# Two state-space layers on one core: scans in another order, one more PSUM bank for the first layer's decays, and an MLP cut by hidden features

## The chip, the core and the metric

One core of a Trainium2 chip runs the whole program. The metric is the device time of one execution in microseconds (us). All data is fp32. The engines are named as the profile names them: PE (matmul) with PEld (its weight loads), DVE (vector), ACT (activations), POOL (GpSimd) and SP, which here only issues DMAs. Each engine works through its own queue in order; an instruction that waits holds up all that is queued behind it.

## The reference, cut to what matters

The input is 8 images of 384 channels and 32 x 32 pixels. Four layers follow each other, each on the group-normalized image, each added to its input. Layers 0 and 2 are selective state-space layers over the 1024 pixels; layer 2 has a layer norm ahead and an MLP behind. Layer 1 is a filter in 8 x 8 patches with a gated depthwise convolution, layer 3 a 3 x 3 depthwise convolution.

```python
x = x + L0(gn(x)); x = x + L1(gn(x)); x = x + L2(gn(x)); x = x + L3(gn(x))

# L0 and L2, for each image: 768 inner channels d, 16 states n, 1024 places t
xin, z = split(xseq @ in_proj.T)
u   = silu(causal_conv3(xin))
dt, B, C = split(u @ x_proj.T)
dt  = softplus(dt @ dt_proj.T + bias)
dA  = exp(dt[:, :, None] * A)                     # the decay
h_t = dA_t * h_(t-1) + (dt_t * u_t) * B_t         # the scan
y_t = sum_n(h_t * C_t) + u_t * D
out = (y * silu(z)) @ out_proj.T

# L2 only
xseq = layer_norm(xseq)                            # ahead of in_proj
out  = gelu(out @ mlp_w1.T + b1) @ mlp_w2.T + b2   # 384 -> 1536 -> 384
```

## The kernel before

**Chunks and steps.** An image's 1024 places are two halves of T = 512, so each of the two state-space layers has 16 chunks. What the code calls `l0_` and `l2_` is here the first and the second layer. A chunk has 24 steps; 32 chunks give 768 steps. A step treats 32 channels with 16 states each, as four groups j = 0 to 3 of 128 partitions x 512 places. The main loop (line 1015) runs over the steps.

**What a step does.** `begin` loads dt * u from DRAM, spread to all 16 states, into a tile g, three steps ahead. `times` multiplies g by B on POOL (L623, two instructions), one step ahead. `decay` copies dt to the states with four matmuls (lhsT `selr`) into four PSUM banks dA0 to dA3 and takes the exponential in place on ACT (L241). `scan` runs four scans on DVE (L643). For j = 0 and 1 the result goes back into the dA bank and DVE multiplies it by C (L654); for j = 2 and 3 it goes into g, and one POOL instruction multiplies both by C (L660). `gather` sums over the states with four matmuls into the bank y, adds u * D with one more matmul in the first layer (the diagonal matrix is loaded once, `w_D`) or on DVE in the second, and multiplies by the gate z on DVE.

**PSUM.** There are eight banks: dA0 to dA3 (`psa`), y (`psy`), and a pool of three (`psg`, tag `ps`) that all other work shares. That work writes a pool tile with matmuls, and an ACT or DVE instruction reads it out, after which the bank is free.

**Other work.** Generators, called jobs, do the rest in pieces: `measure` and the group statistics, `front` (normalization, in_proj as ps_in, the convolution taps on DVE, x_proj, dt as ps_dt), `gates` (ps_z), `out_proj`, `layer1` (ps_t, ps_dw, ps_o1), `mlp` (ps_up, ps_dn) and `layer3`. In each step the loop emits, in this order, `times` of the next step, `scan`, job pieces of up to 2.0 units of PE work, `gather` of the step before, `begin`, more job pieces as long as the budget `ROOM` lasts, and `decay` of the next step. A piece that finds no free pool bank or no lock reports WAIT and is tried later; `jobs.until` forces pieces at once where a step needs their result. As everything is emitted in this order, a DVE instruction of a job stands behind the scans of the step in which it is emitted. Matmuls are emitted by one helper, activations by another, so the profile shows L177 and L241 for nearly all of them, and L85 for DVE work of jobs; the tile names tell them apart.

**dt.** `step_dt` takes a pool bank, computes log(1 + exp(-|x|)) on ACT into a tile `spm`, adds max(x, 0) on DVE, which frees the bank, multiplies by u on POOL into a tile `du`, and spills that to DRAM. `spm` has two buffers, which `measure` (its image blocks `xk`) and `layer_norm` (its squares `sq`) use as well; `live["spm"]` is set while `measure` uses them.

**MLP.** It runs twice over a chunk, for 256 places each time. Each pass needs all weights: 12 loads of 384 KB into four buffers `mw`, so 24 a chunk. A pool bank holds two hidden blocks of 256 places.

Of the kernel before, what the change touches and what calls it, by code (L numbers as in the profile page):

```python
# [47 lines left out]
NBANK = 3  # L48

SHARE = {"l0_": ((2, 2, 2, 2), (2, 2, 2, 2)), "l2_": ((2, 2, 2, 2), (2, 2, 2, 2))}  # L50
# [105 lines left out]
def tile_conv_preact_d4(ctx: ExitStack, tc: tile.TileContext, a: dict, out: bass.AP):  # L156
# [6 lines left out]
    psg = ctx.enter_context(tc.tile_pool(name="psg", bufs=NBANK, space=PSUM))  # L163
# [3 lines left out]
    live = {"ps": 0, "dt": 0, "x": 0, "spm": False}  # L167
# [11 lines left out]
    def ps_tile(name):  # L179

        while live["ps"] >= NBANK:
            yield WAIT
        live["ps"] += 1
        return psg.tile([P, 512], F32, tag="ps", name=name)

    def ps_done():
        live["ps"] -= 1

    def pipe(units, deep=2):
# [4 lines left out]
        while units or flying:  # L194
# [7 lines left out]
            if units and live["ps"] < NBANK and len(flying) < deep:  # L202
                went = True
                name, stages = units.popleft()
                live["ps"] += 1
                ps = psg.tile([P, 512], F32, tag="ps", name=name)
                stages[0](ps)
                f = {"stages": deque(stages[1:]), "ps": ps, "bank": True}
                settle(f)
                if f["stages"]:  # L210
                    flying.append(f)
# [3 lines left out]
    def settle(f):  # L215
        if f["bank"] and (not f["stages"] or f["stages"][0] is None):
            f["bank"] = False
            ps_done()
# [61 lines left out]
    def group_stats(block, all_read=lambda: None, between=None):  # L280
# [15 lines left out]
        def group_mean(v):  # L296
# [11 lines left out]
            return ps[:, 0:KC].unsqueeze(2)  # L308

        ps = yield from group_mean(mv[:, :, 0:1])  # L310
        nmean = wk.tile([P, KC, 1], F32, tag="gnm", name="gnm", bufs=2)
        act(nmean, ps, AF.Copy, scale=-1.0)
        ps_done()
# [5 lines left out]
        ps = yield from group_mean(dv)  # L319
        rstd = wk.tile([P, KC, 1], F32, tag="grstd", name="grstd", bufs=3)  # L320
        rsqrt(rstd, ps, eps_gn)
        ps_done()
# [33 lines left out]
    def load_diagonal(w, pre):  # L356
        w["D"] = wk.tile([P, ND, P], F32, tag="w_D", name="w_D")
        nc.sync.dma_start(w["D"], a[pre + "D"].rearrange("d p q -> p d q"))

# [4 lines left out]
    def depthwise(pool, rows, todo):  # L364
# [13 lines left out]
        for q, (n, t) in enumerate(taps):  # L378
# [8 lines left out]
            if t == 8:  # L387
                take(ps[:rows])
                ps_done()
# [9 lines left out]
    def measure(s):  # L399
# [4 lines left out]
        def load(q):  # L404
            if q < len(blocks):
                h, k = blocks[q]
                x = loaded[h, k] = wk.tile([P, T], F32, tag="spm", name="xk", bufs=2)
# [4 lines left out]
        live["spm"] = True  # L412
# [7 lines left out]
        def all_read():  # L420
            live["spm"] = False
# [38 lines left out]
    def layer_norm(xn):  # L460
# [5 lines left out]
        ps_done()  # L466
        yield NEXT
        while live["spm"]:
            yield WAIT
        ps = yield from ps_tile("ps_lv")  # L470
        for k in range(KC):
            sq = wk.tile([P, T], F32, tag="spm", name="sq", bufs=2)
            act(sq, xn[:, k, :], AF.Square)
            mm(ps, ln_mean, sq, start=k == 0, stop=k == KC - 1)
# [6 lines left out]
        ps_done()  # L481
# [5 lines left out]
    def front(s):  # L487
# [67 lines left out]
        ps_done()  # L555
# [10 lines left out]
        def step_dt(d):  # L566
# [3 lines left out]
            def log(ps):  # L570
                mm(ps, w["dt"][DT0:RX, d * P : (d + 1) * P], dbc[DT0:RX, :])
                v = got["m"] = wk.tile([P, T], F32, tag="spm", name="spm", bufs=2)
# [8 lines left out]
            def times_u(ps):  # L581
                v = got["du"] = wk.tile([P, T], F32, tag="du", name="du", bufs=2)
                nc.gpsimd.tensor_mul(v, s["dt"][d], u[d])

            def spill(ps):
# [3 lines left out]
                for j in range(4):  # L589
                    nc.sync.dma_start(to[:, j, :], got["du"][32 * j : 32 * (j + 1), :])  # L590
# [5 lines left out]
        flying = []  # L596
        for d in range(ND):
            while live["dt"] >= NDT or live["spm"]:
                yield WAIT
            live["dt"] += 1  # L600

            flying.append(pipe([("ps_dt", step_dt(d))]))
            flying = [f for f in flying if next(f, f) is not f]
            yield NEXT
        while flying:
            flying = [f for f in flying if next(f, f) is not f]
            yield NEXT
# [11 lines left out]
    def times(s, i):  # L619

        for j in (0, 2):
# [5 lines left out]
    def decay(s, i):  # L627
        k, sub = QUADS[i]
# [5 lines left out]
        for j in range(4):  # L634
            act(dAs[j], dAs[j], AF.Exp, scale=s["w"]["A"][:, 4 * i + j : 4 * i + j + 1])

    def scan(s, i):

        g = s["g", i]
        own = SHARE[s["pre"]][s["c"]][i % NSUB]  # L640
        for j in range(4):
            q = 4 * i + j
            nc.vector.tensor_tensor_scan(  # L643
                dAs[j] if j < own else g[:, j, :],
                dAs[j],
# [5 lines left out]
            if j < own:  # L651
                if s["c"] < NCH - 1:
                    nc.vector.tensor_copy(carry[:, q : q + 1], dAs[j][:, T - 1 : T])
                nc.vector.tensor_mul(g[:, j, :], dAs[j], s["bc"][:, 1, :])  # L654
        if s["c"] < NCH - 1:
            nc.vector.tensor_copy(  # L656
                carry[:, 4 * i + own : 4 * i + 4].unsqueeze(2), g[:, own:4, T - 1 : T]
            )
        g = g[:, own:4, :]
        nc.gpsimd.tensor_mul(  # L660
            g, g, s["bc"][:, 1, :].unsqueeze(1).to_broadcast([P, 4 - own, T])
        )

    def gather(s, i):
# [6 lines left out]
        for j in range(4):  # L671
            mm(y[32 * j : 32 * (j + 1), :], sely[:, sub, :], g[:, j, :], sub == 0, sub == NSUB - 1 and s["pre"] == "l2_")
        if sub == NSUB - 1:
            u = s["u"][k // NH][:, k % NH, :]
            if s["pre"] == "l0_":
                mm(y, s["w"]["D"][:, k, :], u, start=False)
# [74 lines left out]
    def load_layer1():  # L751
# [14 lines left out]
        ps_done()  # L766
# [95 lines left out]
    TH = T // 2  # L862
# [10 lines left out]
    def weights():  # L873

        parts = [a["l2_mlp_w1"][f : f + 2].rearrange("f p k q -> p f k q") for f in range(0, NF, 2)]
        parts += [
            a["l2_mlp_w2"][m][:, g * NFH : (g + 1) * NFH, :]
            for m in range(KC)
            for g in range(2)
        ]  # L880
        parts = deque(parts + parts)
# [14 lines left out]
    def mlp(s):  # L896
        x = s["x"]
        loaded, more = s["weights"]
        first = True

        def take():

            nonlocal first
            if not first:
                more()
            first = False
# [272 lines left out]
```

## Time and profile before

| | |
|---|---|
| Median of 3 runs | 7783.18 us (7766.74 to 7798.79) |
| The profiled execution | 7774.96 us, span 7773.2 us |
| Granted PE clock, mean | 0.922 |
| PE busy | 7244.1 us (93%) |
| DVE busy | 5787.0 us (74%) |
| POOL busy | 5638.8 us (73%) |
| ACT busy | 4034.0 us (52%) |
| Head, up to the first scan | 95 us |
| First layer, 384 steps | 3453 us |
| Second layer, 384 steps | 4034 us |
| Tail after the last step's first scan | 192 us |

The page is one execution. "Busy" of PE is modelled: a matmul counts from its start to the end of its write, so waits between the matmuls of a group can lie inside it. PEld rows are weight loads; a wait of PE shows there first, since the load precedes the matmul. A row of the waits reads: engine, tile and line that waited, what ended the wait, total us, how often, and the longest. A granted clock of 1.0 is full speed, 0.5 half. The first three rows of matmuls, four 32-row or 32-column matmuls at once, are the dA and y groups; a 512-column fp32 matmul appears as two instructions.

### The profile page before, as it was taken

Reading aid. Unit: us, or ns where it says so; the run is one execution under the profiler, and the core shown is the slowest. Engines: PE = TensorE matmul, PEld = TensorE weight load, DVE = VectorE, ACT = ScalarE, POOL = GpSimd, SP = SyncE. Lnnn points to the kernel's source line nnn. Section 1 sums busy time; section 2 is a strip of 40 time slices with the busy share of each in tenths; the row PEclk is TensorE's granted clock in tenths of the full one; section 3 lists DMA queues with packets and bytes.
Section 4 is the critical chain, followed back from the end, with each engine's and each line's share of the span. In section 5 each row is a group of like instructions: output and inputs, shape, how many; then the busy total and the mean of one; then the engine's idle time right before and its main releaser. Section 6 shows DMA issues by size and latency. Waiting matters only on the chain. (4 is left out here: it accounts for less than half of the span.)

```text
span 7773.2 us, 76689 instructions
## 1 busy us (share of the span) xinstructions
PE 7244.1 (93%) x25762; PEld 3001.0 (39%) x25762; DVE 5787.0 (74%) x7350; ACT 4034.0 (52%) x6980; POOL 5638.8 (73%) x2710
## 2 busy tenths in 40 slices
PE   7989999999999999999999989999999999999998
PEld 2223333333333333333334434444444444444445
DVE  5988788888777878778746765767777677776871
ACT  4445555554554555455545544555555555555543
POOL 5888878788787878778646764767767677676770
PEclk8888889999888999988899999999999999999999
DMA  5666556556565646556536654666656666565662
GB/s 141 141 151 144 138 134 142 136 135 150 127 146 127 141 120 148 128 139 146 129 78 167 174 135 120 165 156 172 165 150 174 155 170 164 149 164 146 171 168 67
DMA packets 288919, 1122.50 MB, mean 144 GB/s; under 512 B 37386, under 2 KB 90970, under 8 KB 190220
## 3 DMA queue, kind: packets, MB, share of 16 engines
q1 hardware_dynamic: 288524, 1117.59, 58.4%
q8 instruction: 204, 3.34, 0.2%
q14 instruction: 191, 1.56, 0.1%
HBM read 1041.96 MB, written 75.50 MB: 144 GB/s over the span
## 5 line engine op out<-in xcount | busy, mean ns | idle before, releaser
L623 POOL TENSOR_TENSOR g<-g,bc 128x1024 f32<-128x1024 f32 x1536 | 3586.8, 2358 | 197.2 <-DMA g<-dud 181.2
L660 POOL TENSOR_TENSOR g<-g,bc 128x1024 f32<-128x1024 f32 x768 | 1806.2, 2352 | 1441.1 <-DVE carry L656 806.6
L241 ACT ACTIVATE dA<-dA,w_A 128x512 f32<-128x512 f32 x3072 | 1860.7, 662 | 1543.3 <-PE dA L177 1530.1
L177 PE MATMUL dA<-dt,selr 32*128 32x512 f32 x6144 | 1573.3, 677 | 70.6 <-DVE g L654 61.9
L643 DVE TENSOR_TENSOR_SCAN dA<-dA,carry,g 128x512 f32<-128x512 f32 x768 | 986.6, 1285 | 616.0 <-issue 275.6
L643 DVE TENSOR_TENSOR_SCAN dA<-dA,g 128x512 f32<-128x512 f32 x768 | 940.6, 1225 | 477.5 <-issue 167.7
L654 DVE TENSOR_TENSOR g<-dA,bc 128x512 f32<-128x512 f32 x1536 | 1053.9, 686 | 29.8 <-DVE dA L643 0.5
L177 PE MATMUL y<-g,sely 128*32 128x512 f32 x6144 | 934.1, 637 | 43.0 <-POOL g L660 37.5
L643 DVE TENSOR_TENSOR_SCAN g<-dA,carry,g 128x512 f32<-128x512 f32 x768 | 940.6, 1267 | 0.0
L643 DVE TENSOR_TENSOR_SCAN g<-dA,g 128x512 f32<-128x512 f32 x768 | 893.3, 1204 | 0.0
L177 PEld LDWEIGHTS dA<-dt,selr 32*128 32x128 f32 x6144 | 470.2, 191 | 984.4 <-DVE g L643 517.3
L177 PE MATMUL ps_dn<-h,mw 128*128 128x256 f32 x2304 | 573.9, 401 | 75.3 <-DMA mw<-in_l_mlp_w 58.6
L177 PE MATMUL ps_up<-t,mw 128*128 128x256 f32 x2304 | 566.8, 394 | 59.0 <-DMA mw<-in_l_mlp_w 44.2
L177 PE MATMUL ps_z<-xf,w_in 128*128 128x512 f32 x1152 | 586.1, 649 | 27.3 <-DVE dt L85 23.6
L177 PE MATMUL ps_in<-xf,w_in 128*128 128x512 f32 x1152 | 566.9, 633 | 27.3 <-DVE u L85 25.5
L177 PE MATMUL ps_dw<-tp,diag 96*96 96x512 f32 x1152 | 572.8, 638 | 15.2 <-ACT diag L241 15.2
L177 PE MATMUL ps_out<-u,w_out 128*128 128x512 f32 x1152 | 543.7, 619 | 10.2 <-DVE x L85 10.2
L177 PEld LDWEIGHTS ps_dn<-h,mw 128*128 128x128 f32 x2304 | 439.5, 197 | 277.0 <-issue 118.8
L177 PEld LDWEIGHTS ps_up<-t,mw 128*128 128x128 f32 x2304 | 425.8, 192 | 268.4 <-issue 148.9
L177 PE MATMUL ps_dw<-xp,diag 128*128 128x512 f32 x864 | 407.5, 622 | 42.2 <-ACT diag L241 40.9
L241 ACT ACTIVATE u<-ps_in,w_vec 128x512 f32<-128x512 f32 x192 | 149.4, 778 | 484.2 <-PE ps_in L177 484.2
L177 PEld LDWEIGHTS y<-g,sely 128*32 128x32 f32 x6144 | 134.2, 111 | 648.5 <-issue 461.1
(99 smaller groups left out, 6463.1 us busy)
## 6 DMA issues: line engine op xcount, KB each, us to landing
g<-dud SPq DMA_DIRECT2D x768, 1024.0 KB, 7.1
mw<-in_l_mlp_w SPq DMA_DIRECT2D x384, 384.0 KB, 7.4
dud<-du SPq DMA_DIRECT2D x768, 64.0 KB, 1.7
xk<-in_x SPq DMA_DIRECT2D x48, 256.0 KB, 4.2
xf<-in_x SPq DMA_DIRECT2D x16, 768.0 KB, 8.4
x<-in_x SPq DMA_DIRECT2D x16, 768.0 KB, 8.5
x_mid<-x SPq DMA_DIRECT2D x16, 768.0 KB, 4.6
xk<-x_mid SPq DMA_DIRECT2D x48, 256.0 KB, 5.0
```

The costliest lines, as they stand in the source:

```text
L177: nc.tensor.matmul(out_, lhsT, rhs, start=start, stop=stop)
L241: nc.scalar.activation(out_, in_, func, **kw)
L623: nc.gpsimd.tensor_mul(g, g, s["bc"][:, 0, :].unsqueeze(1).to_broadcast([P, 2, T]))
L643: nc.vector.tensor_tensor_scan(dAs[j] if j < own else g[:, j, :], dAs[j], g[:, j, :], 0.0 if s["c"] == 0 else carry[:, q : q + 1], ALU.mul ...
L654: nc.vector.tensor_mul(g[:, j, :], dAs[j], s["bc"][:, 1, :])
L660: nc.gpsimd.tensor_mul(g, g, s["bc"][:, 1, :].unsqueeze(1).to_broadcast([P, 4 - own, T]))
```

## The change

Six edits, which belong to three groups.

- **Decays and scans.** The order of groups in a step is now 2, 3, 0, 1 for the exponentials and the scans, and `times` treats j = 2, 3 first. POOL's product by C is emitted right after scan 3. In the first layer the exponential of group 1 is taken last in a step (`decay_last`) and goes from its dA bank into a bank of its own, `dAx` (tag `b2`), where scan 1 and its product work. The matmuls keep the order 0, 1, 2, 3. The pool has two banks, `b0` and `b1`, in the first layer; `b2` joins them after the last step of the first layer. The diagonal of D is made on ACT from the unit matrix, 96 times, and is loaded no more.
- **MLP.** It runs over all 512 places at once and is cut by hidden features: six blocks up, GELU, down into x; then the other six. Each weight is loaded once a chunk. A pool bank holds one hidden block, and a piece is one matmul of 512 columns.
- **Squares and dt.** The three squares of `layer_norm` are taken one step ahead of the matmuls that sum them; `spm` has three buffers, `du` is gone (the product is written into `spm`), and `live["spm"]` names who holds the buffers: `measure`, `squares` or `dt`.

```diff
-NBANK = 3
+OWN = 2
+ORDER = (2, 3, 0, 1)
...
-    live = {"ps": 0, "dt": 0, "x": 0, "spm": False}
+    live = {"dt": 0, "x": 0, "spm": None, "banks": ["b0", "b1"]}
...
+    def bank(name):
+        tag = live["banks"].pop(0)
+        ps = psg.tile([P, 512], F32, tag=tag, name=name)
+        held[id(ps)] = ps, tag
+        return ps
+
+    def ps_done(ps):
+        live["banks"].append(held.pop(id(ps))[1])
...
+        live["spm"] = "squares"
+        sq = [wk.tile([P, T], F32, tag="spm", name="sq", bufs=3) for _ in range(KC)]
+        for k in range(KC):
+            act(sq[k], xn[:, k, :], AF.Square)
+        yield NEXT
         ps = yield from ps_tile("ps_lv")
         for k in range(KC):
-            sq = wk.tile([P, T], F32, tag="spm", name="sq", bufs=2)
-            act(sq, xn[:, k, :], AF.Square)
-            mm(ps, ln_mean, sq, start=k == 0, stop=k == KC - 1)
+            mm(ps, ln_mean, sq[k], start=k == 0, stop=k == KC - 1)
+        live["spm"] = None
...
             def times_u(ps):
-                v = got["du"] = wk.tile([P, T], F32, tag="du", name="du", bufs=2)
-                nc.gpsimd.tensor_mul(v, s["dt"][d], u[d])
+                nc.gpsimd.tensor_mul(got["m"], s["dt"][d], u[d])
...
     def times(s, i):
-        for j in (0, 2):
+        for j in (2, 0):
...
-        for j in range(4):
-            act(dAs[j], dAs[j], AF.Exp, scale=s["w"]["A"][:, 4 * i + j : 4 * i + j + 1])
+        s["dA"] = list(dAs)
+        for j in ORDER:
+            if j != ORDER[-1] or s["pre"] == "l2_":
+                act(dAs[j], dAs[j], AF.Exp, scale=s["w"]["A"][:, 4 * i + j : 4 * i + j + 1])
+
+    def decay_last(s, i):
+        if s["pre"] == "l0_":
+            j = ORDER[-1]
+            s["dA"][j] = psg.tile([P, T], F32, tag="b2", name="dAx")
+            act(s["dA"][j], dAs[j], AF.Exp, scale=s["w"]["A"][:, 4 * i + j : 4 * i + j + 1])
...
     def scan(s, i):
-        for j in range(4):
+        for j in ORDER:
...
-            if j < own:
+            if j < OWN:
                 if s["c"] < NCH - 1:
-                    nc.vector.tensor_copy(carry[:, q : q + 1], dAs[j][:, T - 1 : T])
-                nc.vector.tensor_mul(g[:, j, :], dAs[j], s["bc"][:, 1, :])
-        if s["c"] < NCH - 1:
-            nc.vector.tensor_copy(
-                carry[:, 4 * i + own : 4 * i + 4].unsqueeze(2), g[:, own:4, T - 1 : T]
-            )
-        g = g[:, own:4, :]
-        nc.gpsimd.tensor_mul(
-            g, g, s["bc"][:, 1, :].unsqueeze(1).to_broadcast([P, 4 - own, T])
-        )
+                    nc.vector.tensor_copy(carry[:, q : q + 1], dA[j][:, T - 1 : T])
+                nc.vector.tensor_mul(g[:, j, :], dA[j], s["bc"][:, 1, :])
+            elif j == 3:
+                if s["c"] < NCH - 1:
+                    nc.vector.tensor_copy(
+                        carry[:, 4 * i + OWN : 4 * i + 4].unsqueeze(2), g[:, OWN:4, T - 1 : T]
+                    )
+                r = g[:, OWN:4, :]
+                nc.gpsimd.tensor_mul(
+                    r, r, s["bc"][:, 1, :].unsqueeze(1).to_broadcast([P, 4 - OWN, T])
+                )
...
+        if sub == NSUB - 2 and s["pre"] == "l0_":
+            s["D", k] = wk.tile([P, P], F32, tag="D", name="D")
+            act(s["D", k], eye, AF.Copy, scale=s["w"]["vec"][:, k, 4:5])
...
-                mm(y, s["w"]["D"][:, k, :], u, start=False)
+                mm(y, s.pop(("D", k)), u, start=False)
...
     def weights():
...
+        for g in range(2):
+            for f in range(g * NFH, (g + 1) * NFH, 2):
+                parts.append(a["l2_mlp_w1"][f : f + 2].rearrange("f p k q -> p f k q"))
+            for m in range(KC):
+                parts.append(a["l2_mlp_w2"][m][:, g * NFH : (g + 1) * NFH, :])
...
-        for half in range(2):
-            cols = slice(half * TH, (half + 1) * TH)
-            h1 = p2.tile([P, NF, TH], F32, tag="h1", name="h1")
+        for g in range(2):
+            h1 = p2.tile([P, NFH, T], F32, tag="h1", name="h1")
...
+                def run(k):
+                    def run_k(ps):
+                        if f % 2 == 0 and k == 0:
+                            take()
+                        mm(
+                            ps, now[0][:, f % 2 * KC + k, :], s["t"][k], start=k == 0,
+                            stop=k == KC - 1,
+                        )
...
+                    xm = x[:, m, :]
+                    if g == 0:
+                        vector.scalar_tensor_tensor(
+                            xm, ps, b2[:, m : m + 1], xm, ALU.add, ALU.add
+                        )
+                    else:
+                        vector.tensor_add(xm, ps, xm)
...
         scan(s, i)
+        if t == total // 2 - 1:
+            live["banks"].append("b2")
...
         jobs.step(t)
-        if t + 1 < total:
-            decay(*steps[t + 1])
+        if nxt:
+            decay(*nxt)
+            decay_last(*nxt)
```

## The prediction

> **What bounds the kernel now.** I read the busy rows of the page, then the busy times by stretch (head, first layer, second layer, tail; the cuts are the first scans of the layers), then the waits inside each layer, then the instructions in order of time.
>
> The busy times by stretch, columns PE, PEld, DVE, ACT, POOL, granted clock, DMA:
>
> ```profile
> 95.00:3547.80 3452.80, 3262.05 (x10780) 1131.25 (x10780) 2835.17 (x3561) 1815.44 (x3218) 2810.77 (x1348) 0.90 0.58 138
> 3547.80:7581.50 4033.70, 3758.78 (x14333) 1743.26 (x14332) 2912.64 (x3726) 2122.07 (x3581) 2808.05 (x1343) 0.95 0.61 154
> ```
>
> PE looks full, but its matmuls are modelled to last until they end, stalls included. What it streams can be counted: dense 512-column fp32 matmuls are two instructions whose starts lie 0.43 us apart (0.86 us in all), a quad of dA or y takes 1.07 to 1.13 us. With these the program's PE work is 6.40 us a step in the first layer and 8.34 us in the second, of 9.0 and 10.5 us that a step lasts. DVE does 6.25 us of scans and products in each step and 1.3 to 1.5 us of other work. So PE and DVE are nearly equal, each 70 to 87% used, and the time is lost where they wait for each other. The waits of the first layer, then of the second:
>
> ```profile
> PEld dA L177 <- DVE g L643: 308.6, 430, 1.7
> PEld dA L177 <- DVE g L654: 180.5, 140, 13.1
> PEld ps_z L177 <- DVE dt L85: 34.2, 13, 5.3
> ```
> ```profile
> PEld dA L177 <- DVE g L643: 207.8, 309, 1.7
> PEld ps_lv L177 <- ACT sq L241: 65.8, 43, 4.6
> PE ps_dn L177 <- DMA mw<-in_l_mlp_w: 58.6, 24, 5.6
> PE ps_up L177 <- DMA mw<-in_l_mlp_w: 44.2, 34, 4.8
> PE ps_lv L177 <- ACT sq L241: 37.2, 13, 3.0
> ```
>
> The dA matmuls write over the banks that the scans still read, so PE stands some 490 us in the first layer behind scans and products. In the other direction, DVE idles between the steps for 555 us in the first layer and 1053 us in the second (counted from the end of one step's scans to the first scan of the next, less the DVE work between), nearly all of it ended by the first exponential, thus by a PE that came late. From the first dA matmul to the first scan takes 1.9 us.
>
> One step in order of time, where a bank of the pool is at fault:
>
> ```profile
> 2572.93 2.45 DVE L643 TENSOR_TENSOR_SCAN g<-dA,carry,g 128x512 f32<-128x512 f32 x2
> ...
> 2575.30 0.67 DVE L85 SCALAR_TENSOR_TENSOR dt<-ps_dt,spm 128x512 f32<-128x512 f32 x1
> ...
> 2576.02 5.36 PE L177 MATMUL ps_z<-xf,w_in 128*128 128x512 f32 x6 [4.38 <-DVE dt L85]
> ...
> 2581.31 1.14 PE L177 MATMUL dA<-dt,selr 32*128 32x512 f32 x8
> ...
> 2583.21 1.29 DVE L643 TENSOR_TENSOR_SCAN dA<-dA,carry,g 128x512 f32<-128x512 f32 x1 [6.32 <-POOL g L623]
> ```
>
> ps_z needs the bank that ps_dt held. Its release is the dt addition on DVE, which is queued behind all four scans of the step. PE idles 4.38 us, then works at half speed (six matmuls in 5.36 us instead of 2.6), and only then come the dA matmuls: the step is 14.1 us long. DVE stands from 2576.9 to 2583.2.
>
> **What the Trainium skill says.** "TensorE: Matmul & The Clock Gate", Part 1: after an idle window of about 3.4 us PE runs at half its clock until it has been busy again for about as long. The lines above agree (0.86 us from ps_z to ps_z after 4.38 us idle). "Perfetto Trace Analysis", Matmuls: independent groups should rotate through different PSUM banks so that the eviction of one overlaps the next. "PSUM — Partial Sum Buffer", Specifications: eight banks, each 512 fp32 columns. The kernel has 4 (dA) + 1 (y) + 3 (pool), so the first layer's extra bank can only come out of the pool, which keeps two.
>
> **The change part by part.**
>
> First layer, decays and scans. Now the order on DVE is scan 2, scan 3, scan 0, product 0, scan 1, product 1. dA0 is free after product 0, that is 1.9 us (1.24 + 0.69) before the step's end; dA1 is free once the exponential into the extra bank is done; dA2 and dA3 have long been free. PE can thus pass the dA matmuls up to 1.9 us earlier. Exponential 2 starts 1.16 us after them and scan 2 0.75 us later, just when product 1 ends, so DVE loses nothing. The gather that follows needs product 1; in the changed program's order it comes first in 192 of 382 steps, and there the lead is only the 1.1 us of the quad. Per step, the smaller of PE's present stall, this lead, and the DVE idle time that follows it: 124 us over the layer where the lead is carried from step to step and steps with a bank wait are left out, 171 us with the full lead everywhere. I take -145. The exponential last in the step waits for product 1 on ACT; behind it are the next step's evictions, whose matmuls end later than it does (ACT is 53% busy), so nothing. POOL's product now needs two scans instead of four; POOL is the last to release a step's first scan in 3 of 383 steps, so nothing. The new diagonal on ACT, 96 x 0.40 = 38 us, has a step of room: nothing; without that room at most 38.
>
> Pool of two banks in the first layer, single f per bank in the MLP. In the built order I looked for PE work that stands behind a DVE eviction of its own step, hence behind all its scans, as ps_z above. Before: 15 steps in the first layer and 23 in the second; after: 78 and 68, mostly ps_t, ps_o1 and ps_up behind dt. PE work left behind the wait, up to the dA matmuls: 70 and 153 us before, 270 and 363 after. Such a gap is about that work plus 1.5 us (0.7 eviction + 1.9 - 1.1 for the quad counted). Set against the gap that the same steps have now (they average 3.7 and 4.4 us, so many are late already) this adds 69 + 71 = 140 us. The upper end: steps of this kind lose 4.4 us against 9.0 with 3.6 us of work behind (six, ps_z), 1.3 us with 1.8 (four, ps_t), 1.0 us with 2.4 in the second layer (thirteen, ps_up), half clock included; drawn on to the others it gives about 430. I take +200, nearer the low end, because a PE that is late does not wait.
>
> Order in the second layer. There is no extra bank: dA1 waits for product 1, the end of the step, and dA2 is issued behind it. So each gap is at least 2.0 us, which 97 steps now undercut by 92 us in sum. Some of that meets a late PE: +55 (0 to 92).
>
> MLP. Streaming is equal: 216 ns from start to start for 256 columns, 429 for 512; weight loads run under it. Weights are loaded once, 12 pieces of 384 KB a chunk instead of 24, and each lasts 5.1 us of PE instead of 2.6, so three pieces ahead cover 15 us, over the 7.4 us to landing. The gaps before ps_up and ps_dn with a mark over 0.5 us sum to 128 us; the two DMA lines above hold 103. -110 (80 to 128). Pieces of one matmul fill the steps better: five forced stretches of 32.9 us of PE work become 20.1, three more lose 14 in all, 78 us together; the work moves into steps that are about half full of it: -45 (0 to 78). Evictions: ACT 384 x 0.47 becomes 192 x about 0.65, hidden; DVE 96 adds of 0.47 become 96 of about 0.70, +22 us, half exposed: +10.
>
> Squares a step ahead: three squares of 0.64 us end before PE comes. Idle PE before ps_lv 37 us plus 3 in the first layer: -40 (20 to 65, the weight-load line). The dt buffers (du into spm) and the missing load of w_D lie under other work: nothing, at most 5.
>
> Sum: -145 + 200 + 55 - 110 - 45 + 10 - 40 = -75. The profiled execution took 7774.96 us with a span of 7773.2; the median 7783.18 is 8 above. 7775 - 75 + 5 = 7705.
>
> **The rivals.**
> A, slower: the bank waits decide. Speaking for it: the six ps_z steps, and that PE, when it leads, only waits longer and goes cold. At 430 us the sum is +155: 7935. It decides from 275 us on, which is 2.5 us for each of the 108 added steps. Against it: the 140 us of the first working.
> B, no change: the lead is not used, since in the first layer the next thing PE meets waits for the step's end anyway (half of the steps open with the gather, 65 with ps_dt). 40 instead of 145: sum +30, 7810.
> C, much faster: bank waits at 140, lead carried further with fewer half-clock stretches (these cost 280 us in the first layer now): lead -250, sum -240 with the rest as above: 7545.
>
> **How the numbers follow.** Forecast 0.40, A 0.25, B 0.20, C 0.15. About 0.5% (39 us) is what a measurement of this kernel can tell from no change. The forecast's own range is 7630 to 7760. Faster: most of the forecast's (0.34), all of C, a little of B (0.04): 0.53. Slower: A and 0.04 of B: 0.29. The rest, 0.18, is the same. The range from 7540 to 7940 reaches to C and A.
>
> **What would show it.** Right: PE's waits for scans before dA in the first layer fall from 490 us to under 300, DVE's gap there falls, the mw and ps_lv lines nearly vanish, each layer-two gap is at least 2.0 us. Wrong: PE waits on DVE dt before ps_t, ps_o1 and ps_up grow from tens of us to over 300, with a lower granted clock than 0.90 in the first layer; or the first layer keeps its 3453 us with both lines moved only.

## The result and the profile after

The changed kernel takes 8212.3 us (median of 4 runs, 8203.0 to 8221.3), beside 7779.7 us for the kernel before: ratio 1.0548, 95% interval 1.0526 to 1.0570. It is 5.5% slower. The prediction (7705 us, 7540 to 7940) was wrong.

The profiled execution has a span of 8216.7 us, 443.5 more. By stretch (columns core stretch, PE, PEld, DVE, ACT, POOL, granted clock, DMA share, GB/s; the cuts are again the first scans of the layers):

```profile
93.20:3798.40 3705.20, 3018.50 (x10803) 1045.67 (x10804) 2879.66 (x3566) 1835.46 (x3327) 2815.08 (x1350) 0.86 0.54 129
3798.40:8036.50 4238.10, 3798.22 (x12164) 1330.62 (x12163) 2956.55 (x3720) 2080.99 (x3394) 2802.68 (x1340) 0.92 0.52 129
```

The first layer lost about 250 us (3453 to 3705), the second about 205 (4034 to 4238). DVE's and POOL's busy times hardly moved (DVE about 1.5% more, POOL as before); the granted clock fell in both layers, from 0.90 to 0.86 and from 0.95 to 0.92. So the loss is not work added to DVE or POOL: PE waited more, and then ran more slowly. The waits of the first layer after the change (engine, tile and line, what ended the wait: us in total, times, longest), of PE for DVE:

```profile
PEld dA L176 <- DVE g L671: 404.0, 172, 16.0
PE dA L176 <- DVE g L671: 237.1, 105, 14.4
PEld ps_t L176 <- DVE dt L84: 211.4, 44, 7.6
PE ps_t L176 <- DVE dt L84: 182.0, 44, 7.4
PEld dA L176 <- DVE dAx L660: 54.2, 68, 1.7
```

The same view of the second layer:

```profile
PEld dA L176 <- DVE g L671: 301.3, 264, 9.2
PEld ps_up L176 <- DVE dt L84: 163.7, 37, 6.7
PE ps_up L176 <- DVE dt L84: 133.0, 37, 5.8
```

A stall shows once in PEld (the weight load) and again in PE, so the two rows are not added. The mw and sq lines of before are gone, as predicted. In their place stand ps_t and ps_up behind dt, 182 and 133 us of idle PE, 81 times. The wait before dA in the first layer has hardly shrunk: 404 + 54 us, where it was 309 + 181.

One step of the second layer (16 of an odd chunk), in order of time, columns start, duration, engine, line:

```profile
5897.68 1.28 DVE L660 TENSOR_TENSOR_SCAN dA<-dA,carry,g 128x512 f32<-128x512 f32 x1
...
5899.61 0.68 DVE L84 SCALAR_TENSOR_TENSOR dt<-ps_dt,spm 128x512 f32<-128x512 f32 x1
...
5900.35 2.07 PE L176 MATMUL ps_up<-t,mw 128*128 128x512 f32 x2 [5.84 <-DVE dt L84]
...
5902.35 1.57 PE L176 MATMUL y<-g,sely 128*32 128x512 f32 x8
...
5903.85 3.70 PE L176 MATMUL ps_up<-t,mw 128*128 128x512 f32 x8
...
5907.48 1.14 PE L176 MATMUL dA<-dt,selr 32*128 32x512 f32 x8
...
5909.42 1.28 DVE L660 TENSOR_TENSOR_SCAN g<-dA,carry,g 128x512 f32<-128x512 f32 x1 [3.94 <-ACT dA L246]
```

ps_up needs the bank that ps_dt held. Its release, the dt addition, stands on DVE behind the last scan and product, though its last input, `spm`, was ready 2.7 us before it ran. PE is idle for 5.84 us, starts at half speed (a quad of y in 1.57 us instead of 1.07) and has all its work of the step still ahead, so the next scans begin at 5909.4, 16.0 us after those of the step before. It is the case that the prediction's last fence shows for ps_z, now in 146 steps instead of 38.

These steps carry the whole loss. Matched with the same steps of the trace before, the 78 of the first layer lost 283 us together and the 68 of the second 210 us; all other steps lost nothing (-37 and -4 us). Most of the 493 us, about 440, lies in steps that were not held before. Such a held step lasts 14.2 us on average in the first layer and 15.9 in the second, the others 8.5 and 10.0.

### The profile page after: what moved, and what is told of

Same layout as the page of the kernel before. It is cut to its first block, busy times and chain, and to the rows that moved or that the text cites. A ratio compares the mean times of both kernels' runs of the same rounds, so it can differ in the third digit from the quotient of the medians.

```text
span 8216.7 us, 72178 instructions
## 1 busy us (share of the span) xinstructions
PE 7030.9 (86%) x23458; PEld 2469.6 (30%) x23458; DVE 5876.7 (72%) x7350; ACT 4010.0 (49%) x6884; POOL 5635.7 (69%) x2710
## 3 DMA queue, kind: packets, MB, share of 16 engines
q14 instruction: 192, 1.57, 0.1%
## 5 line engine op out<-in xcount | busy, mean ns | idle before, releaser
L246 ACT ACTIVATE dA<-dA,w_A 128x512 f32<-128x512 f32 x2688 | 1617.2, 660 | 1855.3 <-PE dA L176 1855.0
L176 PE MATMUL dA<-dt,selr 32*128 32x512 f32 x6144 | 1141.8, 710 | 344.5 <-DVE g L671 344.0
L671 DVE TENSOR_TENSOR g<-dA,bc 128x512 f32<-128x512 f32 x1152 | 791.0, 687 | 19.7
L660 DVE TENSOR_TENSOR_SCAN dA<-dA,carry,g 128x512 f32<-128x512 f32 x576 | 732.5, 1272 | 0.0
L176 PE MATMUL ps_up<-t,mw 128*128 128x512 f32 x1152 | 593.9, 648 | 149.2 <-DVE dt L84 133.0
L660 DVE TENSOR_TENSOR_SCAN dA<-dA,g 128x512 f32<-128x512 f32 x576 | 706.1, 1226 | 0.6 <-issue 0.5
L176 PE MATMUL ps_dn<-h,mw 128*128 128x512 f32 x1152 | 572.4, 638 | 26.4 <-DVE dt L84 13.8
L176 PEld LDWEIGHTS ps_up<-t,mw 128*128 128x128 f32 x1152 | 215.2, 202 | 518.0 <-issue 315.7
L84 DVE SCALAR_TENSOR_TENSOR u<-ps_in,w_vec,u 128x511 f32<-128x511 f32 (+1 forms) x384 | 282.4, 746 | 123.4 <-ACT xt L246 88.1
L589 POOL TENSOR_TENSOR spm<-dt,u 128x512 f32<-128x512 f32 x192 | 243.5, 1268 | 175.7 <-DVE dt L84 175.7
```

The lines of the kernel that those rows point to most:

```text
L84: return call(out_, *args, **kw)
L176: nc.tensor.matmul(out_, lhsT, rhs, start=start, stop=stop)
L246: nc.scalar.activation(out_, in_, func, **kw)
L589: nc.gpsimd.tensor_mul(got["m"], s["dt"][d], u[d])
L660: nc.vector.tensor_tensor_scan(dA[j] if j < OWN else g[:, j, :], dA[j], g[:, j, :], 0.0 if s["c"] == 0 else carry[:, q : q + 1], ALU.mult, ...
L671: nc.vector.tensor_mul(g[:, j, :], dA[j], s["bc"][:, 1, :])
```

## The experiments

All kernels here compute the whole reference. "First" and "second" are the two layers in the trace in us: from the first scan of all to the first of the second layer, and from there to the first scan of the last step. (In the trace before, the second layer's first scan lies 4 us behind the cut of the stretches, hence 3457 and 4029 beside 3453 and 4034.) "Held" counts the steps, read from the built order, in which PE work stands behind a DVE eviction of its own step. Ratios are to the kernel before.

| kernel | what it is | us | ratio (95%) | first | second | held |
|---|---|---|---|---|---|---|
| before | | 7776 to 7796 | 1 | 3457 | 4029 | 15, 23 |
| after | all edits | 8212.3 | 1.0548 (1.0526, 1.0570) | 3705 | 4238 | 78, 68 |
| e0 | before, banks by a list | 7820.8 | 1.0063 (1.0038, 1.0087) | 3495 | 4039 | 20, 50 |
| e1 | e0, two banks in the first layer | 8089.4 | 1.0410 (1.0383, 1.0437) | 3763 | 4036 | 78, 50 |
| a3 | after without the extra bank | 8185.3 | 1.0530 (1.0504, 1.0557) | 3668 | 4242 | 21, 68 |
| a4 | a3, dA matmuls in scan order | 7997.3 | 1.0280 (1.0258, 1.0303) | 3521 | 4199 | 21, 68 |
| a5 | after, dt off DVE | 7890.7 | 1.0151 (1.0116, 1.0187) | 3543 | 4069 | 34, 30 |
| a6 | a4, dt off DVE | 7814.0 | 1.0036 (1.0018, 1.0054) | 3511 | 4025 | 5, 30 |
| a9 | a6, banks by rotation | 7807.7 | 1.0025 (1.0013, 1.0036) | 3517 | 4014 | 5, 29 |
| a10 | a9, taps read a copy | 7940.0 | 1.0187 (1.0172, 1.0202) | 3646 | 4028 | 5, 14 |
| b2 | before, MLP edit | 7801.8 | 1.0019 (1.0008, 1.0030) | 3462 | 4033 | 15, 42 |
| b3 | before, order of groups | 7954.2 | 1.0220 (1.0193, 1.0247) | 3648 | 4034 | 11, 23 |
| b5 | before, dt off DVE | 7804.7 | 1.0026 (1.0012, 1.0040) | 3489 | 4021 | 5, 10 |
| b7 | before, squares and dt buffers | 7987.9 | 1.0262 (1.0241, 1.0284) | 3482 | 4233 | 15, 39 |
| b8 | b7, MLP edit | 7822.5 | 1.0048 (1.0030, 1.0066) | 3491 | 4052 | 15, 50 |
| b9 | b8, banks by a list | 7918.5 | 1.0167 (1.0144, 1.0190) | 3503 | 4138 | 21, 68 |
| b11 | b3, dA matmuls in scan order, dt off DVE | 7758.6 | 0.9970 (0.9960, 0.9980) | 3492 | 3988 | 5, 10 |
| b13 | b7, dt off DVE | 8002.0 | 1.0287 (1.0263, 1.0311) | 3493 | 4222 | 5, 24 |
| b14 | b7, squares not moved | 7777.4 | 0.9994 (0.9977, 1.0011) | 3478 | 3998 | 15, 22 |
| b16 | b7, taps read a copy | 8281.9 | 1.0618 (1.0600, 1.0635) | 3691 | 4319 | 15, 23 |

The theory ("bank theory" below) was rival A: the time goes into PE held by a PSUM bank behind DVE's scans. Its rival ("order theory"): the new order of scans costs it.

**The bank alone (e0, e1).** e0 is the kernel before with the changed kernel's way to hand out its three banks (a list, first freed first given). e1 takes one bank away in the first layer.

```diff
-    live = {"dt": 0, "x": 0, "spm": False, "banks": ["b0", "b1", "b2"]}
+    live = {"dt": 0, "x": 0, "spm": False, "banks": ["b0", "b1"]}
...
         scan(s, i)
+        if t == total // 2 - 1:
+            live["banks"].append("b2")
```

> The kernel before, with its pool of three banks handed out by the changed kernel's list (first freed, first given) in both layers; nothing else. Bank theory (PE held behind a DVE eviction of its own step is what costs): in the built order such steps go from 15 to 20 in the first layer and from 23 to 50 in the second, at about 3.3 us each, so about +105 us, 7885 us, all in the second layer. Order theory (the new order of scans and the exponential that is taken last hold up ACT and DVE): nothing of that is here, so 7780 us within 0.3%.

> The kernel before with two pool banks in the first layer and three in the second, by the list; scans, decays, MLP and squares as before. Bank theory: 78 held steps in the first layer as in the changed kernel, 50 in the second: about +280 us in the first layer (3.6 us for each of 63 added steps and what they lengthen) and the +85 of the list in the second, 8130 us. Order theory: 7780 us, at most +40.

The first layer went from 3495 to 3763: the bank costs 268 us for 58 more held steps, 4.6 us each, near the bank theory's 8130 us. The waits of e1 in its first layer, then of e0 in its own:

```profile
PEld ps_t L177 <- DVE dt L85: 197.1, 42, 7.5
PE ps_t L177 <- DVE dt L85: 167.6, 38, 7.3
```
```profile
PEld ps_t L177 <- DVE dt L85: 11.5, 6, 4.0
PE ps_t L177 <- DVE dt L85: 8.4, 4, 3.3
```

One bank less turns 8 us of waiting into 168. Of the 268 us, the 58 steps themselves lost 204, or 3.5 each; the rest lies around them. That e0 itself costs 38 us in the first layer neither theory expected, and in the second layer the bank theory missed: 27 more held steps were to cost 85 us there, and the layer lost 10. Thirteen of them lost nothing: they had lasted 12.2 us before as well. So the number of held steps alone does not set the price.

**The changed kernel without the extra bank (a3), then with its matmuls in the order of the scans (a4), and the order of groups alone (b3).** a3 gives `b2` back to the pool and takes all four exponentials in place; b3 puts the new `scan`, `times` and order of exponentials into the kernel before. The edit of a3, then that of a4 on top:

```diff
-    live = {"dt": 0, "x": 0, "spm": None, "banks": ["b0", "b1"]}
+    live = {"dt": 0, "x": 0, "spm": None, "banks": ["b0", "b1", "b2"]}
...
-            if j != ORDER[-1] or s["pre"] == "l2_":
-                act(dAs[j], dAs[j], AF.Exp, scale=s["w"]["A"][:, 4 * i + j : 4 * i + j + 1])
+            act(dAs[j], dAs[j], AF.Exp, scale=s["w"]["A"][:, 4 * i + j : 4 * i + j + 1])
```

```diff
     def decay(s, i):
-        for j in range(4):
+        for j in ORDER:
             rows = slice(32 * j, 32 * (j + 1))
             mm(dAs[j], selr[rows, sub, :], s["dt"][k][rows, :])
```

> The changed kernel without the extra bank of the first layer: its exponential stays in place, the pool has three banks from the start; order, MLP and squares stay changed. Bank theory: held steps in the first layer fall from 78 to 21, so its 3705 us come down to about 3540 (the 3453 of before, and gaps of at least 2.0 us as in the second layer); the second layer stays at 4238; about 8050 us. Order theory: no gain, 8210 us or more.

> The changed kernel without the extra bank (pool of three, as in a3_no_extra_bank, 8185 us), and the four matmuls of dA issued in the order of the scans, 2, 3, 0, 1. Order theory: dA2 and dA3 are free 1.2 and 2.5 us into the step, so their exponentials are ready when the step ends and the floor of 2.0 us under the gaps goes: -170 us in the first layer, -100 to -170 in the second, 7880 us. Rival (the floor hardly matters since PE is late anyway): within 40 us of 8185.

> The kernel before with the new order of groups (exponentials, scans, POOL's product early) in both layers, no extra bank, the matmuls of dA still 0 to 3. Order theory: scan 2 of a step cannot start before dA2, which is issued behind dA1, which waits for the step's last product; every gap is at least 2.0 us. The first layer without the extra bank stands 173 us above the list of three, so +170 there and +100 to +170 in the second layer: about 8080 us. Rival (prediction's step: 92 us of shortfall in the second layer and 152 in the first, much of it meeting a late PE): +100 us or less, 7880 us.

a3 is near the order theory's number: without its own bank the new order is no gain in the first layer but a loss, 3668 (b3 3648), although the held steps fell to 21. The reason stands in a3's waits of that layer:

```profile
PEld dA L176 <- DVE g L670: 740.3, 462, 16.1
PE dA L176 <- DVE g L670: 338.5, 223, 14.7
```

The matmuls kept the order 0, 1, 2, 3, so dA2, which the next step scans first, is issued behind dA1, which waits for the last product. Every gap between two steps, from the last product to the next scan, is at least 1.98 us; the 25th percentile is no more than that. In a4 that row falls to `442.1, 393, 3.7` and the first layer to 3521, 147 us less, near the 170 expected. So the extra bank, at 268 us, removes a wait that one reordered loop removes without a bank. In the second layer the order theory was wrong: b3 costs 5 us there and a4 brings 43, where 100 to 170 were expected of each.

**dt off DVE (a5; a6 with a4's edits; b5 on the kernel before).** The maximum goes to ACT, the addition to POOL. The bank is then free without DVE, and DVE has 192 instructions less.

```diff
                 act(v, ps, AF.Abs)
+                r = s["dt"][d] = wk.tile([P, T], F32, tag="dt", name="dt", bufs=NDT)
+                act(r, ps, AF.Relu)
...
-                v = s["dt"][d] = wk.tile([P, T], F32, tag="dt", name="dt", bufs=NDT)
-                vector.scalar_tensor_tensor(v, ps, 0.0, got["m"], ALU.max, ALU.add)
+                v = s["dt"][d]
+                nc.gpsimd.tensor_add(v, v, got["m"])
```

> The changed kernel, with max(x, 0) of dt taken by ACT straight from the bank and the addition done on POOL, so that no bank of dt waits for DVE. ACT gets 192 x 0.6 us and POOL 192 x 1.27 us more, DVE 192 x 0.68 less. Bank theory: held steps fall from 78 to 34 and from 68 to 30, at 3.3 us each about -270 us: 7940 us, and the waits of PE for dt vanish. Order theory: no gain, 8210 us or, with a fuller POOL, more.

> The kernel before with max(x, 0) of dt on ACT and the addition on POOL; nothing else. Held steps fall from 15 to 5 and from 23 to 10. Bank theory: the six ps_z steps lose 4.4 us each, the others 1.0 to 1.3, so -45, and 131 us less on DVE, half of it exposed: -100 in all, 7680 us. Rival (POOL's later addition delays the spill and with it the loads of g): 7780 us or more.

> The one before (a4_matmuls_in_order) with dt taken off DVE as in a5_dt_off_dve. If both theories hold and add up: 7880 us less about 160 for the second layer and 60 or more for the first (few held steps are left there), 7650 us, under the kernel before. If the bank waits were the whole of it, no better than a5_dt_off_dve's first layer with three banks: about 7800 us.

a5 takes 322 us off the changed kernel, 162 in the first layer and 169 in the second; b5, the same edit on the kernel before, where few steps are held, takes nothing off (the bank theory had 7680 us there and missed). So it is not the lighter DVE that helps, but the bank: this decides for rival A. The ps_up group of the changed kernel and of a5 (busy and mean ns; idle just before, and what ended it):

```profile
L176 PE MATMUL ps_up<-t,mw 128*128 128x512 f32 x1152 | 593.9, 648 | 149.2 <-DVE dt L84 133.0 <-DVE xf L84 7.5 <-DVE u L84 4.9
```
```profile
L176 PE MATMUL ps_up<-t,mw 128*128 128x512 f32 x1152 | 563.2, 624 | 40.4 <-ACT dt L246 23.9 <-DVE xf L84 7.5 <-DVE u L84 4.9
```

133 us of waiting become 24. a6 reaches 7814 us: not the 7650 of two gains that add up, but about the 7800 expected if the bank waits were the whole of it.

**The MLP alone (b2).** The whole MLP part of the change on the kernel before.

```diff
-        for half in range(2):
-            cols = slice(half * TH, (half + 1) * TH)
-            h1 = p2.tile([P, NF, TH], F32, tag="h1", name="h1")
+        for g in range(2):
+            h1 = p2.tile([P, NFH, T], F32, tag="h1", name="h1")
```

> The kernel before with the changed MLP alone (all 512 places, weights once). Prediction's step: -110 for the weights' DMA and -45 for the smaller forced stretches, +10 for the adds, so about -145 if no bank waits come with it: 7630 us. Bank theory as it stands now (held steps with little work behind them cost next to nothing in the second layer, those with 5 us and more cost 6.7): held steps go from 23 to 42, of which some ten with over 5 us of work behind, so +65 of that is lost: 7700 us. Rival: the MLP alone makes the second layer slower, over 7790 us.

Nothing: +0.2%, as the rival had it. The waits for mw, 103 us before, are gone, and five even chunks in the middle of the second layer fall from 267 to 248 us on average (the forced step 3 from 42.1 to 29.5; in one of the five, from 312 to 254, lies 58 us of it). But the odd chunks rise from 234 to 255 us. There steps 10 to 13 last 17.7, 15.5, 15.8 and 13.0 us instead of 9.1, 9.1, 10.5 and 6.7. The waits of the second layer in b2, then of before, name what is met there:

```profile
PE ps_in L177 <- DVE u L85: 54.0, 28, 4.9
```
```profile
PE ps_in L177 <- DVE u L85: 17.8, 27, 3.8
```

`u` is what the convolution taps on DVE write, reading the bank ps_in. Step by step, all odd chunks lost 107 us and all even ones gained 103. Ten newly held steps in which ps_in stands behind the taps lost 75 us, fourteen in which ps_up does lost 33.

**Squares and dt buffers alone (b7), then with the MLP (b8) and with the list (b9).** b7 is the third group of the change on the kernel before; its core:

```diff
+        live["spm"] = "squares"
+        sq = [wk.tile([P, T], F32, tag="spm", name="sq", bufs=3) for _ in range(KC)]
+        for k in range(KC):
+            act(sq[k], xn[:, k, :], AF.Square)
+        yield NEXT
         ps = yield from ps_tile("ps_lv")
```

> The kernel before with the edits to squares and dt buffers alone (squares a step ahead, three spm buffers with one holder, du in spm). Prediction's step: -40: 7740 us. Coincidence theory (the second layer's loss comes from steps in which dt and the MLP's or front's units meet, so that PE is held with 3.6 us and more behind it; alone each edit makes few of them): held steps in the second layer 23 to 39, the added ones with 3.6 us behind at some 3 us each, -40 + 45: 7785 us, same. Rival (the new lock on spm alone makes the second layer late): over 7900 us.

> The edits to squares, dt buffers and MLP together, the pool of three still handed out in turn, no new order. Coincidence theory: held steps in the second layer 23 to 50, of which one per odd chunk (step 16) with 6.4 us behind: about +60, 7845 us. Rival (edits add up: squares about 0, MLP +4): 7790 us.

> The one before with the three banks handed out by the changed kernel's list; still no new order and no extra bank. Held steps in the second layer 68, the same as in the changed kernel, with steps 16, 17 and 18 of each odd chunk in a row with 6.4 to 7.3 us behind. Coincidence theory: the second layer is as slow as in the changed kernel (4238), the first as with the list (3495): 8020 us. Rival (edits add up: +45 for the list): 7840 us.

The edit that was to bring 40 us costs 204 in the second layer when made alone, only 23 together with the MLP, 109 with the list as well, and 213 with the order on top (a3): the edits do not add up. b7 is as slow as the rival had it (over 7900 us); b8 and b9 lie between their two expectations. Each edit shifts pieces of the jobs and thus changes what meets the scans and which bank a tile gets.

**Which part of it (b13, b14).** b13 is b7 with dt off DVE. b14 keeps the lock, the three buffers and du in spm, but leaves the squares in the step of their matmuls:

```diff
         ps = yield from ps_tile("ps_lv")
         for k in range(KC):
-            sq = wk.tile([P, T], F32, tag="spm", name="sq", bufs=2)
+            sq = wk.tile([P, T], F32, tag="spm", name="sq", bufs=3)
```

> The kernel before with the squares, lock and dt buffers of the change, and dt's max on ACT and its addition on POOL. In the squares-alone kernel 29 steps of the second layer hold PE work behind a DVE instruction that they do not hold in the kernel before: 15 times in_proj (ps_in) behind the convolution taps, 11 times ps_up, mostly behind dt. Taps theory: only the ps_up cases go, the 15 ps_in cases stay at 15 us a step; 15 x 5.5 = 82 us and what follows from them stay: about 7900 us (second layer 4130). Theory that dt's bank is all there is: second layer back near 4030, about 7800 us.

> The kernel before with the lock that names its holder, three spm buffers and du written into spm, but with the squares where they were, in the step of their matmuls. If the squares' step ahead moves in_proj behind the taps: as before, 7785 us. If the lock or the buffers cost the time: 7985 us, as with the whole edit.

b14 costs nothing, so the squares' step does it; my rival, the lock, falls, although b7 met its number. b13 is as slow as b7 (8002 us, where even the taps theory had 7900), so dt's bank is not the cause there. In b7, too, steps 10 to 12 of the odd chunks last 14.7 to 15.5 us, and the trace shows why for step 11:

```profile
5583.30 2.45 DVE L650 TENSOR_TENSOR_SCAN g<-dA,carry,g 128x512 f32<-128x512 f32 x2
...
5585.66 1.51 DVE L85 SCALAR_TENSOR_TENSOR u<-ps_in,w_vec,u 128x511 f32<-128x511 f32 x2
...
5587.32 5.46 PE L177 MATMUL ps_in<-xf,w_in 128*128 128x512 f32 x6 [3.83 <-DVE u L85]
...
5592.71 1.33 PE L177 MATMUL dA<-dt,selr 32*128 32x512 f32 x8
...
5595.14 1.28 DVE L650 TENSOR_TENSOR_SCAN dA<-dA,carry,g 128x512 f32<-128x512 f32 x1
```

The pattern is the same as with dt, with another tenant of the bank: the two convolution taps on DVE read ps_in, queued behind the scans. The 15 added steps of this kind in b7 grew from 9.6 to 15.1 us, 82 us together; 14 other added ones lost 47, all remaining steps 74. The built programs show what moved. Steps 10 to 12 of such a chunk hold the same six in_proj matmuls each before and in b7, but before, the two tiles of a step lie in two banks; in b7 both lie in one, so the second waits for the taps that read the first. In the whole second layer, 27 of 69 in_proj tiles that directly follow another one share its bank in b7 and in b13, which is as slow; 3 of 75 before and in b14. With the MLP edit as well (b8) it is 9 of 62, and the loss falls to 23 us.

**The taps read a copy (b16 on b7; a10 on a9, which is described below).** ACT copies the bank into SBUF. b16 also makes D on ACT, for room.

```diff
                 act(u[d], ps, AF.Identity, scale=vec[:, d, 2:3], bias=vec[:, d, 3:4])
+                x = xi[d] = wk.tile([P, T], F32, tag="xi", name="xi", bufs=2)
+                act(x, ps, AF.Copy)
...
-                        u[d][:, j:T], ps[:, 0 : T - j], vec[:, d, 2 - j : 3 - j],
+                        u[d][:, j:T], xi[d][:, 0 : T - j], vec[:, d, 2 - j : 3 - j],
```

> The squares-alone kernel (7987.93 us), with one more ACT instruction per in_proj tile, which copies the bank ps_in into an SBUF tile; the two taps on DVE read the copy, so the bank is free after ACT. The order of all other instructions stays. (For room in SBUF the diagonal of D is made on ACT as in the change.) If the bank behind the taps causes the loss: 15 held steps of ps_in go and what follows from them, second layer near 4040, about 7800 us. If the loss lies elsewhere (a step that simply has too much work after the squares moved): 7990 us or, with the extra work on ACT, 8010.

> All edits without the extra bank, dA matmuls issued 2, 3, 0, 1, rotating pool, dt's addition off DVE (7807.69 us so far), and the taps reading a copy: 5 and 14 steps hold PE work behind DVE instead of 5 and 29. If the gains that the prediction gave the MLP and the squares (110 + 45 + 40 us) were only hidden by the waits for banks: about 7650 us. If these waits' removal is worth just the 15 steps x 4 us, and the MLP's and squares' gains are not on the path that sets the end: 7750 us. If the copies on ACT cost as much as they free: 7810 us.

Both failed, for a reason in neither expectation. The taps in b7, then in b16:

```profile
L85 DVE SCALAR_TENSOR_TENSOR u<-ps_in,w_vec,u 128x511 f32<-128x511 f32 (+1 forms) x384 | 282.3, 745 | 170.0 <-ACT xt L241 136.3 <-ACT u L241 26.8
```
```profile
L85 DVE SCALAR_TENSOR_TENSOR u<-xi,w_vec,u 128x511 f32<-128x511 f32 (+1 forms) x384 | 694.0, 1820 | 83.6 <-ACT xi L241 76.7
```

With both tensors in SBUF one tap takes 1.82 us instead of 0.75, 412 us more on DVE. A stretch of b16 shows where the time goes:

```profile
5619.67 2.35 POOL L667 TENSOR_TENSOR g<-g,bc 128x1024 f32<-128x1024 f32 x1 [1.80 <-DVE carry L663]
...
5621.54 3.79 DVE L85 SCALAR_TENSOR_TENSOR u<-xi,w_vec,u 128x511 f32<-128x511 f32 x2 [2.02 <-ACT xi L241]
5621.97 5.57 POOL L630 TENSOR_TENSOR g<-g,bc 128x1024 f32<-128x1024 f32 x2
```

Two taps that begin while POOL's products run take 3.79 us together instead of 1.5. All 224 slow taps of b16 (over 0.85 us) began inside one of POOL's products over g and ended 0.55 us after its end; so did all 140 of a10. In b7, where the taps read the bank, 233 of the 384 began inside such a product, and none took more than 0.76 us. PE's wait of ps_in for u is gone in b16, but what it cost can't be read from this run. That it explains all of b7's 204 us is not shown.

**What remains once the waits are few (a9, b11).** a9 is a6 with the banks handed out by rotation; b11 is the kernel before with the order of groups, the matmuls in the same order, and dt off DVE.

> All edits without the extra bank, dA matmuls issued 2, 3, 0, 1, dt's addition off DVE, and the three pool banks handed out by rotation in place of the list. If the 38 us that the list cost in the first layer are due to the hand-out: 7814 - 38 = 7775 us. If not: 7814 us, as with the list.

> The kernel before with the new order of groups, dA matmuls issued in the same order 2, 3, 0, 1, and dt's addition off DVE; old MLP and squares. Few steps hold PE work behind DVE (5 and 10). If the order of scans with its banks free early gives PE a lead: dA2 and dA3 are free some 4 us before a step's end, first layer 3489 - 60 = 3430, about 7745 us. If a lead of PE is worth nothing because DVE's own work fills the steps: 7805 us, as with dt off DVE alone.

a9 equals a6 within their intervals, and its first layer (3517) is no better: the 38 us of the list are not a price of the list as such. b11, 7758.6 us, is the fastest of the kernels that were run, 0.3% below the kernel before, its gain in the second layer (3988). That it lies near the expected 7745 is luck: the lead in the first layer, predicted again at 60 us, does not appear (3492 against 3489 in b5).

## Why the prediction was wrong

The failed step is "Pool of two banks in the first layer, single f per bank in the MLP. [...] I take +200, nearer the low end, because a PE that is late does not wait." The steps newly held after the change lost about 440 us, close to the 430 of rival A, which the prediction had given less weight. That is half of the miss. The other half: the remaining terms of the sum make -275, and by the same matching of steps nearly nothing of it came.

- **Counting was right, pricing was wrong.** The 78 and 68 held steps were counted from the built order, and they are the ones that lost. A held step cost 4.6 us in the first layer (e1), above the 2.5 us from which A decides. The working had the gap of DVE grow by 69 us over 63 added steps and 71 over 45, that is 1.1 and 1.6 us each. In the trace the gap of the newly held steps (64 and 49, as some of those held before no longer are) grew by 4.0 us in the first layer (2.9 to 6.9) and by 3.7 in the second (3.7 to 7.5). Two things were mis-sized. These steps were less late before than the 3.7 and 4.4 us of the working, so there was less lateness to hide in. And PE comes out of the wait cold: in the step shown above, work of 6.5 us at full speed took 8.3. Six steps of the ps_z kind had already shown the price before, at 4.4 us each.
- **The price follows the work behind the wait.** Counted without the dA quad, newly held steps with under 2 us of PE work behind the wait lost 3.2 us each in the first layer and 1.0 in the second; those with over 3.5 us lost 7.8 and 7.2.
- **The named sign appeared.** PE's waits for dt before ps_t and ps_up are 182 + 133 = 315 us, over 300, and the clock of the first layer is 0.86, below 0.90. (ps_o1, in the waits `ps_o` without its number, waited for x, 30 us, not for dt.) "TensorE: Matmul & The Clock Gate", Part 1, of the Trainium skill has PE at half clock after an idle window of about 3.4 us; the step shown agrees. Half-clock time, summed from the traces, went from 1207 to 1745 us. PE counts as busy in 1101 and 1427 us of it, so the slower clock itself can account for at most half of the 326 us between, some 160 (an estimate from these sums); most of the loss is waiting.
- **"First layer, decays and scans: -145"** failed as rival B said. With the bank spent (e1, 3763), all the rest of the change brings 58 us in that layer (3705); the wait before dA, to fall under 300 us, is 458. So A and B both came, the bank waits and a lead that is hardly used; the forecast treated them as alternatives. (Rival C's sum comes to 7540 us, not 7545; nothing rests on it.)
- **"Order in the second layer: +55"** was right in its mechanism: no gap of the second layer is under 1.98 us. Alone it costs 5 us there (b3), on top of the others 104 (b9 to a3, 4138 to 4242), of which reordered matmuls recover 43 (a4).
- **"MLP: -110" and "-45"**: the DMA waits vanished as said, and the even chunks gained 103 us in all. The odd chunks gave it back, in the steps in which PE met the taps (b2). The step had put this gain on the path that sets the end without asking what is late next.
- **"Squares a step ahead: -40"**: alone +204 in the second layer. The squares were priced by the wait that they remove, not by where the pieces after them land. About 82 us of it lie in steps whose second in_proj tile got the bank of the first; the rest is not settled.

The sum also fails as a sum: b7 +204, b2 +4, e0 +10 and b3 +5 in the second layer make +223, near the 209 measured, but in steps (b8, b9, a3) the same edits give +23, +109 and +213.

## What to carry to other kernels

Before an edit takes a PSUM bank away or moves work between steps, list every bank's releasing instruction and what is queued ahead of it on that engine; if it stands behind the step's long work, price it by the PE work behind it, the first part of which ran at half clock in the step shown: here 1 to 3 us a step with under 2 us of work behind, 7 to 8 with over 3.5, and nothing where the step was as late before. Issue matmuls in the order in which their results are consumed before spending a bank on freeing them early. In a program that packs job pieces into steps, a gain of one edit is not its own: compare the built order of the whole and the bank that each tile gets, and look for a saved wait at the next bank.

## What the runs showed that was not expected

- A DVE scalar_tensor_tensor of 128x511 with one tensor in PSUM took 0.75 us, whatever POOL did; with both in SBUF 1.82 us on average: 42% of them about 0.75, half of them over 2.5, each slow one ending 0.55 us after a POOL product of 128x1024 (2.35 us alone) during which it had begun. "SBUF — State Buffer", in "SBUF: two separate sides", of the Trainium skill says that a DVE instruction with two SBUF inputs and a GpSimd instruction that reads SBUF lock a shared port for the whole instruction, and the later one waits; these numbers agree.
- Three banks given out by a list instead of by rotation cost 38 us of 3457 in the first layer with nothing else changed, but nothing once dt is off DVE (a6 3511, a9 3517).
- Moving three 0.64 us squares one step earlier cost 204 us, and in the built program it put successive in_proj tiles into one bank.
